# Two PSUM tiles for exp in a selective scan: given out by the framework, or fixed by even and odd number

## The chip, the cores and the metric

The kernel runs on one core of one Trainium2 chip. The core has five engines with instruction queues of their own: TensorE (PE, with its weight loads as PEld), VectorE (DVE), ScalarE (ACT), GpSimd (POOL) and SyncE (SP), which here only issues DMA transfers. Each engine works through its queue in order, and waits on semaphores for what other engines produce or set free. The metric is the device time of one execution in microseconds; lower is better.

## The reference, cut to what matters

The input x has the shape 2 x 256 x 256 x 128. The first layer is a row attention; the second is a state space layer with a selective scan. Only the second matters here. Each image has L = 65,536 positions, 256 inner channels and 16 states per channel:

```python
dA = jnp.exp(delta[:, :, :, None] * A[None, :, None, :])
dBx = (delta * xs)[:, :, :, None] * jnp.transpose(Bs, (0, 2, 1))[:, None]
...
def step(h, inp):
    dA_t, dBx_t, c_t = inp
    h = dA_t * h + dBx_t
    return (h, jnp.einsum('bdn,bn->bd', h, c_t))
...
y = jnp.moveaxis(ys, 0, 2)
return y + Ds[None, :, None] * xs
```

For each channel and state there is a first-order recurrence along the positions: h = dA * h + dBx. The output is the sum over states of h times C. Around it lie a projection, a 3 x 3 depthwise convolution, silu, softplus, a layer norm, a gate and an output projection.

## The kernel before

An image is cut into 64 steps of 4 rows, T = 1024 positions, so that there are 128 steps. In a step the 256 channels x 16 states are 4096 recurrences, 128 partitions of which make a unit: NU = 32 units a step. A unit t goes through these pieces:

```python
POOLED = (4, 7, 10, 13, 16, 19, 24, 26, 31)
...
ps_d = ctx.enter_context(tc.tile_pool(name="ps_d", bufs=2, space=PSUM))
...
def pooled(t):
    return t % NU in POOLED

def decay(t):                                   # ScalarE: da = exp(delta * A), into PSUM
    k, h, m, q = unit(t)
    da = units[t]["da"] = ps_d.tile([P, T], F32, name="da")
    g = h * NQ + q
    nc.scalar.activation(
        da, spreads["delta", k, h, q], AF.Exp, scale=a_neg[:, g, m : m + 1]
    )

def drive(t):                                   # GpSimd: hb = (delta * x) * B, into SBUF
    ...
    hb = s5.tile([P, T], F32, name="hb")
    nc.gpsimd.tensor_tensor(hb, spreads["du", k, h, q], repeats["bb", k, h, m], ALU.mult)

def scan(t):                                    # VectorE: the recurrence
    ...
    u["h"] = u["hb"] if pooled(t) else u["da"]  # written over one of its inputs
    nc.vector.tensor_tensor_scan(u["h"], u["da"], u["hb"], st, ALU.mult, ALU.add)

def remember(t):                                # ScalarE: the last position, for the next step
    ...
    nc.scalar.copy(st, units[t]["h"][:, T - 1 : T])

def product(t):                                 # h * C, on GpSimd for nine units of 32
    ...
    u["yc"] = s8.tile([P, T], F32, name="yc")
    eng = nc.gpsimd if pooled(t) else nc.vector
    eng.tensor_tensor(u["yc"], u["h"], repeats["cc", k, h, m], ALU.mult)
```

A tile da is 128 x 1024 in fp32[...]. [...]in the nine pooled units the scan writes over hb in SBUF, and GpSimd takes the product. In these units da is used up when the scan ends. In the other 23 the scan writes over da, and da is in use until the product and the copy of the last position are done.

The loop sets the order of the queues; what a line below issues stands in its engine's queue in this order:

```python
for t in range(min(slots), max(slots) + 1):
    if 0 <= t + AHEAD < end:
        fetch(t + AHEAD)
    ...
    if 0 <= t + 2 < end:
        drive(t + 2)
    if 0 <= t - 1 < end and pooled(t - 1):
        product(t - 1)
    if 0 <= t + 1 < end:
        decay(t + 1)
    if 0 <= t < end:
        scan(t)
        if not pooled(t):
            product(t)
    if 0 <= t - 5 < end and (t - 5) % NQ == 0:
        add_up(t - 5)    # PE: sums yc over the states
    if 0 <= t - 6 < end and unit(t - 6)[2:] == (NSG - 1, 0):
        y_out(t - 6)     # ScalarE: copies the sum out
    for piece, args in slots.pop(t, ()):
        piece(*args)
    if 0 <= t < end:
        remember(t)
```

The `slots` hold the other work, spread over the units: for the step after the next the projection, convolution (`conv`, `conv_out`, line 515), gate (`gate`, `gate_out`, line 540), silu, B and C (`states`), delta (`size`, `softplus`), and for the step before the layer norm (`turn`: yt, `stats`, `scales`: rstd, `norm`, `back`, `affine`), the gate (`gated`: yg), the output projection (`mix`: o_ps) and its exit (`leave`: ob). ScalarE takes all evictions of these from PSUM. Softplus and silu use another activation table than exp does: a table load stands ahead of each and another one after it.

Of the kernel before, what the change touches and what calls it, by code (L numbers as in the profile page):

```python
# [8 lines left out]
F32 = mybir.dt.float32  # L9
# [3 lines left out]
PSUM = bass.MemoryType.PSUM  # L13
DRAM = bass.MemoryType.DRAM

P = 128
# [5 lines left out]
def attn_then_ssm_kernel(  # L22
# [108 lines left out]
    with tc.tile_pool(name="prep", bufs=1) as prep, tc.tile_pool(  # L131
        name="prep2", bufs=3
# [95 lines left out]
    with tc.tile_pool(name="st", bufs=2) as stp, tc.tile_pool(  # L228
        name="st_x", bufs=3
# [179 lines left out]
    T = R * W  # L409
# [11 lines left out]
    s3 = ctx.enter_context(tc.tile_pool(name="s3", bufs=3))  # L421
    s5 = ctx.enter_context(tc.tile_pool(name="s5", bufs=5))
    s8 = ctx.enter_context(tc.tile_pool(name="s8", bufs=8))
    ps_d = ctx.enter_context(tc.tile_pool(name="ps_d", bufs=2, space=PSUM))
    ps_y = ctx.enter_context(tc.tile_pool(name="ps_y", bufs=1, space=PSUM))
    ps_p = ctx.enter_context(tc.tile_pool(name="ps_p", bufs=1, space=PSUM))
    ps_f = ctx.enter_context(tc.tile_pool(name="ps_f", bufs=1, space=PSUM))
# [312 lines left out]
    units = {}  # L740

    def unit(t):

        k, i = divmod(t, NU)
        h, i = divmod(i, NM)
        m, q = divmod(i, NQ)
        return k, h, m, q
# [26 lines left out]

    def decay(t):
        k, h, m, q = unit(t)
        da = units[t]["da"] = ps_d.tile([P, T], F32, name="da")
        g = h * NQ + q
        nc.scalar.activation(  # L779
            da, spreads["delta", k, h, q], AF.Exp, scale=a_neg[:, g, m : m + 1]  # L780
        )
# [70 lines left out]
    with tc.manual_schedule(engines=engines):  # L852
# [3 lines that stand above are left out]
            if 0 <= t < end and t % (NU * NSTEP) == 0:  # L856
                st = s1.tile([P, NCG, NSG], F32, name="state")
                nc.gpsimd.memset(st, 0.0)
                states_of[steps[t // NU][0]] = st
# [11 lines that stand above are left out]
                add_up(t - 5)  # L871
            if 0 <= t - 6 < end and unit(t - 6)[2:] == (NSG - 1, 0):
                y_out(t - 6)
# [4 lines that stand above are left out]
# [37 lines left out]
```

## Time and profile before

| | |
|---|---|
| time, median of 3 | 18009.35 us (18005.79 to 18027.44) |
| profiled span | 17983.9 us |
| DVE busy | 15218.5 us, 85% |
| PE busy | 14262.3 us, 79% |
| POOL busy | 13400.1 us, 75% |
| ACT busy | 11112.9 us, 62% |
| mean granted TensorE clock | 0.906 of full speed |
| start of the first and of the last scan | 3,497.9 and 17,923.1 us |

The shares mix two parts. Until about 3,500 us the first layer runs, with GpSimd nearly idle; then the 128 steps of the scan follow, with DVE and POOL near full. Within the scan stage (3,490 to 17,930 us, 14,440 us long) DVE is busy for 13,247 us, POOL for 13,358, PE for 11,152, and ACT for 9,567. Busy times count from an instruction's start to its end, and neighbours overlap by up to 0.1 us, so that an engine without gaps shows a little over 100%.

In the groups of instructions, a row holds the line, the engine and the operation, out<-in with shapes and count, then busy time and the mean of one in ns, and last the idle time of the engine just before these instructions with what ended most of it.

### The profile page before, as it was taken

The numbers are of one execution on the slowest core, as the hardware profiler recorded it, in microseconds if no ns is written. First come the engines' busy times: TensorE is split into PE (matmuls) and PEld (weight loads), VectorE is DVE, ScalarE is ACT, GpSimd is POOL, SyncE is SP. The second block draws the span as 40 slices with busy tenths as digits, with TensorE's granted clock in tenths as the row PEclk, the third lists the DMA queues.
The fourth block names the chain that finished last, engine by engine and source line by source line (L and its number), as shares of the span: only waits on it lengthen the run. The fifth ranks groups of instructions, "written<-read, shape, count | busy, mean of one in ns | idle before, by whom it ended". The sixth has DMA issues, their size and how long they took to land. (4 is left out here: it accounts for less than half of the span.)

```text
span 17983.9 us, 178799 instructions
## 1 busy us (share of the span) xinstructions
PE 14262.3 (79%) x56375; PEld 6982.8 (39%) x56375; DVE 15218.5 (85%) x12864; ACT 11112.9 (62%) x19870; POOL 13400.1 (75%) x7084
## 2 busy tenths in 40 slices
PE   4999999777777777777777777777777777777776
PEld 3666666433333333333333333333333333333333
DVE  6555555499999999999999999999999999999998
ACT  2444444466666666666666666666666666666665
POOL 0000000299999999999999999999999999999998
PEclk7999999888899999999999888889888899999887
DMA  4122122266666666666666666666666666666664
GB/s 190 65 71 71 57 71 71 92 220 218 218 221 220 221 221 221 221 221 221 220 220 221 221 219 219 220 220 221 221 220 218 219 221 220 220 220 220 220 219 170
DMA packets 1426641, 3452.04 MB, mean 192 GB/s; under 512 B 119788, under 2 KB 710936, under 8 KB 1407256
## 3 DMA queue, kind: packets, MB, share of 16 engines
q1 hardware_dynamic: 1416984, 3373.49, 54.7%
q0 software_dynamic: 8704, 67.11, 0.9%
q8 instruction: 443, 7.26, 0.2%
q14 instruction: 510, 4.18, 0.1%
HBM read 2752.28 MB, written 687.88 MB: 191 GB/s over the span
## 5 line engine op out<-in xcount | busy, mean ns | idle before, releaser
L787 POOL TENSOR_TENSOR hb<-du_r,bb 128x1024 f32<-128x1024 f32 x4096 | 9566.1, 2360 | 0.0
L794 DVE TENSOR_TENSOR_SCAN da<-da,state,hb 128x1024 f32<-128x1024 f32 x2944 | 6912.4, 2348 | 1064.3 <-ACT da L779 749.3
L779 ACT ACTIVATE da<-delta_r,a_neg 128x1024 f32<-128x1024 f32 x4096 | 4575.5, 1117 | 1155.2 <-DVE hb L794 1086.4
L504 PE MATMUL u_ps<-xn,w_tap 128*128 128x512 f32 x9216 | 4218.6, 603 | 332.3 <-ACT sz L540 242.8
L806 DVE TENSOR_TENSOR yc<-da,cc 128x1024 f32<-128x1024 f32 x2944 | 3605.0, 1225 | 254.2 <-DVE da L794 4.6
L806 POOL TENSOR_TENSOR yc<-hb,cc 128x1024 f32<-128x1024 f32 x1152 | 2714.5, 2356 | 818.9 <-issue 411.9
L794 DVE TENSOR_TENSOR_SCAN hb<-da,state,hb 128x1024 f32<-128x1024 f32 x1152 | 2697.4, 2342 | 15.6 <-ACT da L779 15.3
L826 PE MATMUL y<-yc,sel 128*32 128x512 f32 x16384 | 2469.9, 671 | 280.5 <-POOL yc L806 274.1
L504 PEld LDWEIGHTS u_ps<-xn,w_tap 128*128 128x128 f32 x9216 | 1710.5, 192 | 2348.3 <-issue 1764.8
L398 POOL DMA_DIRECT2D x<-x1g x32 | 23.2, 725 | 3035.0 <-DVE x1g L366 3035.0
L656 PE MATMUL yt<-centre,ys 128*128 128x256 f32 x4096 | 1226.0, 452 | 798.1 <-ACT ob L726 797.0
L799 ACT COPY state<-da 128x1 f32<-128x1 f32 x2944 | 461.2, 157 | 2209.2 <-DVE yc L806 2206.7
L656 PEld LDWEIGHTS yt<-centre,ys 128*128 128x128 f32 x4096 | 895.4, 226 | 1200.8 <-ACT ob L726 992.0
L691 PE MATMUL yd<-ident,yn 128*128 128x128 f32 x2048 | 382.0, 317 | 1126.6 <-ACT yn L680 955.7
L826 PEld LDWEIGHTS y<-yc,sel 128*32 128x32 f32 x16384 | 477.0, 115 | 1973.1 <-issue 1263.9
L552 PE MATMUL xd_ps<-xs,w_xp 128*64 128x512 f32 x1024 | 602.2, 720 | 314.9 <-ACT state L799 174.4
L691 PEld LDWEIGHTS yd<-ident,yn 128*128 128x128 f32 x2048 | 273.3, 160 | 1407.7 <-ACT yn L680 993.9
L570 PE MATMUL dt_ps<-xd,w_dt 8*128 8x512 f32 x1024 | 608.5, 675 | 191.0 <-ACT xd L565 184.1
L515 ACT ACTIVATE xs<-u_ps,cb_c 128x512 f32<-128x512 f32 x512 | 349.6, 683 | 617.8 <-PE u_ps L504 342.5
L318 ACT ACTIVATE e<-s_ps,nmx 128x256 f32<-128x256 f32 x1024 | 472.5, 473 | 355.1 <-DVE nmx L314 354.6
L598 POOL TENSOR_TENSOR xs<-delta,xs 128x1024 f32<-128x1024 f32 x256 | 603.7, 2358 | 40.5 <-ACT delta L589 39.2
L716 PEld LDWEIGHTS o_ps<-w_out,yg 128*128 128x128 f32 x4096 | 604.7, 212 | 35.6
(134 smaller groups left out, 18144.6 us busy)
## 6 DMA issues: line engine op xcount, KB each, us to landing
bb<-bc_d SPq DMA_DIRECT2D x1024, 512.0 KB, 4.2
cc<-bc_d SPq DMA_DIRECT2D x1024, 512.0 KB, 5.2
delta_r<-delta_d SPq DMA_DIRECT2D x1024, 512.0 KB, 5.6
du_r<-du_d SPq DMA_DIRECT2D x1024, 512.0 KB, 4.1
xs_d<-xs SPq DMA_DIRECT2D x128, 1024.0 KB, 3.9
xr<-xs_d SPq DMA_DIRECT2D x256, 512.0 KB, 5.1
delta_d<-delta SPq DMA_DIRECT2D x128, 1024.0 KB, 7.2
du_d<-xs SPq DMA_DIRECT2D x256, 512.0 KB, 3.1
```

Source lines behind the costliest of these rows:

```text
L504: nc.tensor.matmul(o["u"], w_tap[:, h, 3 * dy + dx, :], o["xn"][:, i * RB + dy : i * RB + dy + RB, dx : dx + W], start=(dy == 0 and dx == ...
L552: nc.tensor.matmul(o["xd_ps"], w_xp[:, h, :], o["xs"][:, h, i * TB : (i + 1) * TB], start=(h == 0), stop=(h == NH - 1),)
L570: nc.tensor.matmul(o["dt"], w_dt[:, h, :], o["xd"][0:DR, i * TB : (i + 1) * TB], start=True, stop=True,)
L598: nc.gpsimd.tensor_tensor(du, o["delta"][:, h, :], du, ALU.mult)
L656: nc.tensor.matmul(o["yt"][:, j, :], ys[k, h][:, t0 + j * P : t0 + (j + 1) * P], centre[:, (1 - h) * P : (1 - h) * P + DI], start=(h == 0) ...
L691: nc.tensor.transpose(o["yd"][:, h, j * P : (j + 1) * P], o["yn"][:, j, h * P : (h + 1) * P], ident,)
L716: nc.tensor.matmul(o["o"][:, j, :], o["yg"][:, h, j * P : (j + 1) * P], w_out[:, h, :], start=False, stop=(j == WT - 1 and h == NH - 1),)
L779: nc.scalar.activation(da, spreads["delta", k, h, q], AF.Exp, scale=a_neg[:, g, m : m + 1])
L787: nc.gpsimd.tensor_tensor(hb, spreads["du", k, h, q], repeats["bb", k, h, m], ALU.mult)
L794: nc.vector.tensor_tensor_scan(u["h"], u["da"], u["hb"], st, ALU.mult, ALU.add)
L806: eng.tensor_tensor(u["yc"], u["h"], repeats["cc", k, h, m], ALU.mult)
L826: nc.tensor.matmul(y[q * CQ : (q + 1) * CQ, cols], sel, units[t + q]["yc"][:, cols], start=False, stop=(m == NSG - 1),)
```

## The change

Before, both tiles da come from a pool with two buffers under one name; when a unit asks for one, the framework gives it a buffer that it holds to be free. After the change there are two names with one buffer each, da0 for units of even number and da1 for odd ones, so that a unit always follows the one two before it in its buffer, and the two always alternate. PSUM use stays the same.

```diff
-    ps_d = ctx.enter_context(tc.tile_pool(name="ps_d", bufs=2, space=PSUM))
+    ps_d = ctx.enter_context(tc.tile_pool(name="ps_d", bufs=1, space=PSUM))
...
-        da = units[t]["da"] = ps_d.tile([P, T], F32, name="da")
+        da = units[t]["da"] = ps_d.tile([P, T], F32, name=f"da{t % 2}")
```

It is meant to let the exp of a unit be computed while the scan of the unit before still runs on the other tile.

## The prediction, made before the changed kernel was run

> **What bounds the kernel now.** I read the page first: busy shares, then the 40 slices, then the costliest groups. The page as a whole says that VectorE is the fullest engine, and the slices say where to look: from slice 10 on (about 3,500 us) VectorE and GpSimd are both at 9. That is the scan stage; the ones before it belong to the attention part, which the change does not touch.
>
> ```profile
> PE 14262.3 (79%) x56375; PEld 6982.8 (39%) x56375; DVE 15218.5 (85%) x12864; ACT 11112.9 (62%) x19870; POOL 13400.1 (75%) x7084
> DVE  6555555499999999999999999999999999999998
> POOL 0000000299999999999999999999999999999998
> L787 POOL TENSOR_TENSOR hb<-du_r,bb 128x1024 f32<-128x1024 f32 x4096 | 9566.1, 2360 | 0.0
> L794 DVE TENSOR_TENSOR_SCAN da<-da,state,hb 128x1024 f32<-128x1024 f32 x2944 | 6912.4, 2348 | 1064.3 <-ACT da L779 749.3
> L779 ACT ACTIVATE da<-delta_r,a_neg 128x1024 f32<-128x1024 f32 x4096 | 4575.5, 1117 | 1155.2 <-DVE hb L794 1086.4
> ```
>
> There are 4096 scans, 32 in each of 128 steps. The row to look at is the scan into da: 1064.3 us of idle VectorE before it, ended by ScalarE. And the exp (line 779) itself sat 1086.4 us behind a scan into hb. ScalarE waits for VectorE, and then VectorE for ScalarE: that is a handshake in series, not a full engine. The list of VectorE's waits, cut to the scan stage (3,490 to 17,930 us; columns: total us, times, longest), confirms it:
>
> ```profile
> DVE da L794 <- ACT da L779: 749.3, 514, 149.3
> DVE da L794 <- ACT state L799: 313.5, 249, 1.6
> DVE hb L794 <- ACT da L779: 15.3, 12, 2.0
> ```
>
> The first line holds one wait of 149.3 us, the start of the stage; without it the three lines come to 928.8 us. The timeline shows one such wait, VectorE first, then ScalarE in the same microseconds (columns: start, duration, in brackets the idle before and its releaser):
>
> ```profile
> 9038.63 1.23 DVE L806 TENSOR_TENSOR yc<-da,cc 128x1024 f32<-128x1024 f32 x1
> 9039.77 2.34 DVE L794 TENSOR_TENSOR_SCAN hb<-da,state,hb 128x1024 f32<-128x1024 f32 x1
> 9043.36 2.36 DVE L794 TENSOR_TENSOR_SCAN da<-da,state,hb 128x1024 f32<-128x1024 f32 x1 [1.25 <-ACT state L799]
> ...
> 9040.55 0.59 ACT L540 COPY sz<-z_ps 128x512 f32<-128x512 f32 x1 [1.93 <-PE z_ps L529]
> 9041.03 0.17 ACT L799 COPY state<-da 128x1 f32<-128x1 f32 x1
> 9042.14 1.12 ACT L779 ACTIVATE da<-delta_r,a_neg 128x1024 f32<-128x1024 f32 x1 [0.95 <-DVE hb L794]
> 9043.20 0.17 ACT L799 COPY state<-hb 128x1 f32<-128x1 f32 x1
> ```
>
> The scan of unit 7 (into hb, since 7 is in POOLED) ends at 9042.11. Only then does the exp of unit 8 start; it ends at 9043.26, and scan 8 starts 0.10 later. The wait is booked on the state copy, which ended near it, but its length is that of the exp. Where nothing is missing, the next scan starts 2.26 us after the start of a scan into hb (9030.35 to 9032.61); here it is 3.59. So one such wait costs 1.33 us.
>
> I then numbered the scans of the whole stage by unit and summed the waits over 0.3 us: unit 0 155 us (124 times), 8 157 (125), 11 158 (126), 14 157 (125), 20 158 (126), 23 116 (125), all others 26: together 928. A step takes 112.77 us (median), and five of its units pay 1.25 us each, one 0.93.
>
> [...] the state copy, which only reads da, waits for the product, which only reads it too (ScalarE's waits: 2206.7 us, 1727 times). [...] GpSimd's product takes 2360 ns throughout[...]
>
> **The change part by part.** No instruction is added, and the order on ScalarE, VectorE, PE and GpSimd stays[...]. In the program as built before, the exp of units 8, 11, 14 and 20 of each step, and of unit 0 (in nearly every step), gets the tile of the unit just before it: 626 times in all. Those units follow 7, 10, 13, 19 and 31, all pooled: their da is free when their scan ends, and the framework hands that one out again. After the change no exp does that. The 626 exps wait for the state copy of two units earlier, which is ahead of them on ScalarE; the wait for the scan moves to the copy of hb, after the exp. The 626 are the five units of the table.
>
> What each unit gains, from the step that starts at 9015.52:
> - Units 11, 14, 20: the copies before their exps end at 9050.82, 9062.13 and 9082.86, and the scans they ran behind end at 9053.48, 9064.19 and 9084.92. An exp needs 1.12, so it is hidden with at least 0.7 us to spare. Gain 3 x 1.33 = 4.0.
> - Unit 8: the copy ends at 9041.20 (it stood behind an eviction that waited for PE). The exp would run to 9042.35, scan 8 to start at 9042.45 rather than 9043.36. Gain 0.9; 0.4 stays.
> - Unit 0: behind softplus, its table loads and two evictions the copy ends at 9125.93. The exp would run to 9127.07, the scan start at 9127.17 instead of 9128.16. Gain 1.0; 0.35 stays.
> - Unit 23: two table loads, a silu of 1.91 us and two exps lie in series; this is not the change's matter. But the block begins behind stats, which wait for PE's yt, which waits for the row before to leave (ob); that leaves behind exp 20, earlier now. My choice: 0.3.
>
> Sum 6.2 us a step. Against it I set 0.2, an allowance: PE's stretch from 9023.4 to 9081.2 holds only 3.8 us of idle, VectorE wants it 4 us shorter, and two evictions (units 13 and 14) would then come within 0.1 to 0.7 us of delaying an exp. Net 6.0, so a step of 106.8. Times 128 steps: 768 us. 18009 - 768 = 17241; **predicted 17,240 us**.
>
> **The rivals.**
> - GpSimd becomes the bound. Its work in a step: 32 products at 2.325 when back to back (four took 9.30), 74.4; 9 more for pooled units, 20.9; 2 for du, 4.6; four pairs for rstd, 4.0; copies and memsets, 1.2: 105.1 us. VectorE without any wait: 112.64 - 5 x 1.33 - 0.92 = 105.1 too. So neither can go below 105.1, a gain of 7.7 x 128 = 980 us and 17,030 us. In my walk hb is ready at least 2.2 us before its scan (3.6 now) in every unit. Against it as the bound: at 106.8 GpSimd still has 1.7 us of slack a step.
> - PE becomes the bound through ScalarE's evictions. For: PE is the engine with hardly a gap between units 2 and 18, and ScalarE holds exps behind evictions in one queue; a lower granted clock (0.90 now) would sharpen it. Against: PE waits freely later in the step (5.26 us at 9086.4). If units 8, 14, 15 and 16 each lost 0.4 us more, the step would be 108.4 and the time 17,450.
> - The waits are only moved: the exp no longer waits for the scan, but something else lets ScalarE reach it just as late. For: that is so in part at units 0 and 8. Against: at 11, 14 and 20 ScalarE stood idle for 2.7, 2.1 and 2.1 us before the exp, with nothing but the scan to wait for. If all else failed these three alone make 4.0 x 128 = 510 us, 17,500.
> - Transfers: the stage moves 219 GB/s with its DMA engines busy 0.64 of the time; 6% more is small, and VectorE has no wait on a DMA in the list. No change.
>
> **Range and chances.** Low end: the floor of 17,030 plus a little, since two engines that both run at 105.1 cannot both be free of waits: 17,080. High end: the PE rival, 17,450. Slower than 17,650 (2%) would need over half of the gain to vanish, though the three largest gains have 0.7 us or more to spare: 5%. Slower by 2% would need a new wait of some 9 us a step (360 us over 128 steps, after the gain is gone): 1%.
>
> **What the new profile should show.** If right: the exp's idle behind "DVE hb L794" falls from 1086.4 to under 100 us; idle before the scan into da falls from 1064.3 to 250 to 400 (149 of it the start), what is left standing at units 0, 8 and 23; the state copy takes over waits on the scan into hb; scan, exp and product keep their mean times; GpSimd's idle before its yc falls from 818.9 to under 400. Steps come at 106 to 107 us. Wrong, if scan means grow (then overlap has a cost of its own), if VectorE waits for GpSimd's hb (first rival), or if ScalarE's evictions wait longer for PE and new waits show at units 12 to 17 (second).

## The result, and the profile after

The changed kernel takes **17251.17 us** (median of 4 runs, 17216.71 to 17265.45) against 18009.42 us for the kernel before on the same chip: a ratio of 0.9574, 95% interval 0.9558 to 0.9591. That is 4.3% faster; the prediction said 17,240 us.

From the page of the changed kernel, the busy shares, then two rows of the 40 slices, then the groups (busy us and mean ns of one, then the idle time before them and its main releaser):

```profile
PE 14319.6 (83%) x56375; PEld 6940.5 (40%) x56375; DVE 15182.0 (88%) x12864; ACT 11143.6 (65%) x19870; POOL 13393.4 (78%) x7084
DVE  6555555489999999999999999999999999999998
POOL 0000000089999999999999999999999999999998
...
L794 DVE TENSOR_TENSOR_SCAN da<-da,state,hb 128x1024 f32<-128x1024 f32 x2944 | 6904.3, 2345 | 324.7 <-ACT da L779 321.5
L779 ACT ACTIVATE da<-delta_r,a_neg 128x1024 f32<-128x1024 f32 x4096 | 4576.9, 1117 | 88.7 <-ACT state L799 0.8
...
L806 POOL TENSOR_TENSOR yc<-hb,cc 128x1024 f32<-128x1024 f32 x1152 | 2718.9, 2360 | 201.8 <-issue 156.4
L794 DVE TENSOR_TENSOR_SCAN hb<-da,state,hb 128x1024 f32<-128x1024 f32 x1152 | 2697.9, 2342 | 70.3 <-ACT da L779 70.3
```

The work of one instruction stays within 4 ns: scan 2345 (2348 before), exp 1117 in both, GpSimd's product 2360 (2356). What went is idle time. The exp no longer waits for a scan into hb at all (1086.4 us before), and the idle before the scan into da fell from 1064.3 to 324.7. But the scan into hb, which had 15.6 us, has 70.3: that was not expected. In VectorE's waits of the scan stage (total us, times, longest):

```profile
DVE da L794 <- ACT da L779: 321.5, 319, 151.4
DVE hb L794 <- ACT da L779: 70.3, 38, 2.4
```

Of the first line one wait of 151.4 us is the start of the stage. The rest by unit, in us over the whole stage, start left out; what was predicted to be left stands between. Waits of 0.1 us or more count here. The prediction counted those over 0.3, which would hide unit 0 after the change, where nearly all of 121 waits are shorter:

| unit | before | predicted left | after |
|---|---|---|---|
| 0 | 155 | 45 | 32 |
| 8 | 157 | 51 | 67 |
| 11, 14, 20 | 473 | 0 | 0 |
| 23 | 116 | 80 | 0 |
| 15, 16 (allowance) | 0 | 26 | 0 |
| 28 to 31 | 26 | 26 | 143 |
| sum | 928 | 228 | 243 |

So the sum came out right, though two rows that were put wrong cancel: unit 23 lost its wait altogether, and units 28 to 31 got one. A step now takes 105.98 us in the median (112.77 before) and 107.11 in the mean (112.80): 36 of 127 steps take 108 to 112 us, nearly all others 105.7 to 106.4. The mean difference, 5.70 us, times 128 steps is 730 us; the two profiled executions differ by 720. (The first scan of the kernel before starts at 3,494.3 us; the 3,497.9 in its table is the second.)

Unit 8 in the timeline of the changed kernel, VectorE, then ScalarE (start, duration, in brackets the idle before and its releaser):

```profile
8660.79 2.34 DVE L794 TENSOR_TENSOR_SCAN hb<-da,state,hb 128x1024 f32<-128x1024 f32 x1
8663.45 2.36 DVE L794 TENSOR_TENSOR_SCAN da<-da,state,hb 128x1024 f32<-128x1024 f32 x1 [0.32 <-ACT da L779]
...
8661.57 0.59 ACT L540 COPY sz<-z_ps 128x512 f32<-128x512 f32 x1 [1.93 <-PE z_ps L529]
8662.05 0.17 ACT L799 COPY state<-da 128x1 f32<-128x1 f32 x1
8662.25 1.12 ACT L779 ACTIVATE da<-delta_r,a_neg 128x1024 f32<-128x1024 f32 x1
```

The exp now starts 0.03 after the copy of two units earlier, with scan 7 still running until 8663.13. What is left is the gate eviction (line 540) ahead of it, which waits for TensorE.

### The profile page after: what moved, and what is told of

Its sections match the earlier page's. It is cut to its first block, busy times and chain, and to the rows that moved or that the text cites. A ratio compares the mean times of both kernels' runs of the same rounds, so it can differ in the third digit from the quotient of the medians.

```text
span 17263.7 us, 178676 instructions
## 1 busy us (share of the span) xinstructions
PE 14319.6 (83%) x56375; PEld 6940.5 (40%) x56375; DVE 15182.0 (88%) x12864; ACT 11143.6 (65%) x19870; POOL 13393.4 (78%) x7084
## 5 line engine op out<-in xcount | busy, mean ns | idle before, releaser
L794 DVE TENSOR_TENSOR_SCAN da<-da,state,hb 128x1024 f32<-128x1024 f32 x2944 | 6904.3, 2345 | 324.7 <-ACT da L779 321.5
L779 ACT ACTIVATE da<-delta_r,a_neg 128x1024 f32<-128x1024 f32 x4096 | 4576.9, 1117 | 88.7 <-ACT state L799 0.8
L806 POOL TENSOR_TENSOR yc<-hb,cc 128x1024 f32<-128x1024 f32 x1152 | 2718.9, 2360 | 201.8 <-issue 156.4
L794 DVE TENSOR_TENSOR_SCAN hb<-da,state,hb 128x1024 f32<-128x1024 f32 x1152 | 2697.9, 2342 | 70.3 <-ACT da L779 70.3
L826 PE MATMUL y<-yc,sel 128*32 128x512 f32 x16384 | 2528.0, 681 | 236.9 <-POOL yc L806 230.1
L656 PE MATMUL yt<-centre,ys 128*128 128x256 f32 x4096 | 1068.2, 406 | 226.4 <-ACT ob L726 225.4
L552 PE MATMUL xd_ps<-xs,w_xp 128*64 128x512 f32 x1024 | 687.2, 809 | 480.9 <-ACT state L799 373.1
L656 PEld LDWEIGHTS yt<-centre,ys 128*128 128x128 f32 x4096 | 791.6, 200 | 608.4 <-ACT ob L726 390.2
L570 PE MATMUL dt_ps<-xd,w_dt 8*128 8x512 f32 x1024 | 690.1, 757 | 261.3 <-ACT xd L565 254.4
L699 ACT ACTIVATE yd<-yd,lnb_c,lng_c 128x256 f32<-128x256 f32 x1024 | 542.8, 530 | 149.2 <-PE yd L691 127.8
```

Source lines behind the costliest of these rows:

```text
L552: nc.tensor.matmul(o["xd_ps"], w_xp[:, h, :], o["xs"][:, h, i * TB : (i + 1) * TB], start=(h == 0), stop=(h == NH - 1),)
L570: nc.tensor.matmul(o["dt"], w_dt[:, h, :], o["xd"][0:DR, i * TB : (i + 1) * TB], start=True, stop=True,)
L656: nc.tensor.matmul(o["yt"][:, j, :], ys[k, h][:, t0 + j * P : t0 + (j + 1) * P], centre[:, (1 - h) * P : (1 - h) * P + DI], start=(h == 0) ...
L699: nc.scalar.activation(o["yd"][:, h, :], o["yd"][:, h, :], AF.Identity, bias=lnb_c[:, h : h + 1], scale=lng_c[:, h : h + 1],)
L779: nc.scalar.activation(da, spreads["delta", k, h, q], AF.Exp, scale=a_neg[:, g, m : m + 1])
L826: nc.tensor.matmul(y[q * CQ : (q + 1) * CQ, cols], sel, units[t + q]["yc"][:, cols], start=False, stop=(m == NSG - 1),)
```

## Experiments on the cause

Times are medians, and ratios are to the kernel before on the same chip. Differences in us are between medians from different chips, on which the kernel before took 17,994 to 18,012 us; the four executions of the changed kernel themselves spread over 49 us, and waits by unit come from one execution each. In the first four runs a rule in `decay` chooses the tile:

```diff
+    REPEAT = (0, 8, 11, 14, 20)     # differs from run to run
+    which = {-1: 1}
-        da = units[t]["da"] = ps_d.tile([P, T], F32, name=f"da{t % 2}")
+        which[t] = which[t - 1] if t > 0 and t % NU in REPEAT else 1 - which[t - 1]
+        da = units[t]["da"] = ps_d.tile([P, T], F32, name=f"da{which[t]}")
```

**The old order under the new names** (`REPEAT = (0, 8, 11, 14, 20)`).

> Two names with one buffer each, as in the changed kernel, but units 0, 8, 11, 14 and 20 of every step take the tile of the unit just before them, as they did in the kernel before. If the order of the two tiles at these five units is the whole effect, the time is that of the kernel before: 18,009 us, within 30. If the way the pool gives tiles back (two buffers under one name against two names) has a part of its own, it stays clearly below, under 17,950.

18019.9 us (17998.2 to 18061.36); ratio 1.0009 (1.0002 to 1.0016). The whole gain is the order of the tiles at five units of 32. The 0.1% over the kernel before fits the count: this rule makes 639 repeats, the framework had made 626, and 13 x 1.33 is 17 us.

**Four more repeats** (all nine units after a pooled one).

> As the changed kernel, but after all nine pooled units the next one takes the same tile: 0, 5, 8, 11, 14, 17, 20, 25, 27. Theory: each repeat puts one exp in series, and the four new ones (5, 17, 25, 27) have exps that are on time now, so each costs 1.33 us: 18,009 + 4 x 1.33 x 128 = 18,690 us. Rival: the framework picked this tile where it cost nothing to wait, or other engines' slack takes it up: 18,009 to 18,300 us.

18873.71 us, ratio 1.0482 (1.0466 to 1.0498). The four new waits came as expected, at units 5, 17, 25 and 27, each 1.25 us in every step, and the scan starts 3.60 us after the one before it in place of 2.26. The exp's row of that kernel shows all nine:

```profile
L783 ACT ACTIVATE da<-delta_r,a_neg 128x1024 f32<-128x1024 f32 x4096 | 4579.5, 1118 | 2407.9 <-DVE hb L798 2357.3
```

The cost is larger than the 681 us of the four: against the run with five repeats it is 854. Some 135 us of the rest are longer waits at units 29 to 31 (59 us there with five repeats, 194 here). They go with the granted TensorE clock: between scans 25 and 29 it was below 0.70 in 86 of 124 steps here, and in 15 with five repeats, and those 86 steps hold all but 0.3 us of the waits. What such a clock does there is the subject of the next section. The rival, that other engines' slack takes new repeats up, is wrong.

**Repeats at units 0 and 8 only.**

> As the changed kernel, but units 0 and 8 take the tile of the unit before. Theory: at these two a part of the wait was never the tile's, as ScalarE reaches the exp late in any case; they give back only what they gained, 0.99 and 0.93 us: 1.92 x 128 = 246 us, 17,497 us. Rival: what is left at 0 and 8 after the change is a new wait, and a repeat costs the full 1.34 at each on top: 343 us, 17,594 us.

17424.44 us, ratio 0.9678 (0.9664 to 0.9692), 173 us over the changed kernel where 246 were expected and the rival said 343. By unit the theory holds: unit 0 got 127 us back and unit 8 97 us, with 3.60 us from scan to scan again at both. But the waits at 28 to 31 were 103 us in this execution, not 143. Whether a slower VectorE leaves them less, or this is chance from one execution to the next, is not shown.

**A repeat at unit 20 only.**

> As the changed kernel, but unit 20 of each step takes the tile of unit 19. Theory: scan 20 starts 1.34 us later (3.60 for 2.26 after scan 19), and the wait at unit 23 of some 0.95 us, gone after the change, comes back with it, because the row's exit (ob) stands behind exp 20 on ScalarE, yt behind ob, stats behind yt, and the silu block behind stats: 2.29 us a step, 293 us, 17,544 us. Rival: the wait at 23 went for another reason, as PE ran at another clock there: 1.34 x 128 = 172 us, 17,423 us, and no wait at 23.

17396.63 us, ratio 0.9665 (0.9648 to 0.9681): 145 us over the changed kernel, well under the theory's 293. It is under the rival's 172 too, but by no more than the intervals leave open. The profile has three parts: unit 20 waits 161 us (1.26 in each step), unit 23 waits again, but only in 81 of 128 steps, 60 us in all, and units 28 to 31 wait 49 us instead of 143. Both the theory and the rival for unit 23 thus hold in part, and TensorE's timeline shows how. First yt (turn, in slot 19) in the kernel before, then in the changed kernel, then in two steps of this run:

```profile
9086.43 3.65 PE L656 MATMUL yt<-centre,ys 128*128 128x256 f32 x8 [5.26 <-ACT ob L726]
```

```profile
8913.13 1.99 PE L656 MATMUL yt<-centre,ys 128*128 128x256 f32 x8 [1.16 <-ACT ob L726]
```

```profile
8847.40 3.38 PE L656 MATMUL yt<-centre,ys 128*128 128x256 f32 x8 [3.24 <-ACT ob L726]
...
9063.46 1.99 PE L656 MATMUL yt<-centre,ys 128*128 128x256 f32 x8 [3.23 <-ACT ob L726]
```

The eight matmuls are the same. After 5.26 us of idle TensorE they took 3.65 us, after 1.16 us 1.99. Before the change they took 3.4 to 3.8 us in all of 124 steps in which they start behind scan 20; after it they took 1.99 in 124 of 127. After 3.23 us they took anything from 1.99 to 3.78. The granted clock follows: in the four rows above it was 0.54, 1.00, 0.58 and 1.00 while yt ran.

In the scan stage of the changed kernel the granted clock is 1.0 or 0.5 and nothing else, and all of its 846 changes lie on one grid of 3.41 us. In the run with the repeat at unit 20, the place on its grid goes with what yt takes after 3.23 us: 1.99 us in all 21 steps where yt starts 1.5 to 1.95 us after a grid point, 3.37 to 3.78 in all 41 where it starts up to 1.15 us after one. Stretches at 0.5 came behind gaps of 3.23 us in that run, and behind gaps of 2.3 to 2.7 in the changed kernel (further below).

That yt causes the wait shows step by step: unit 23 waits in none of the 21 steps in which yt took 1.99 us, and 0.8 us on average in the 54 in which it took 3.45 or more. So unit 23 gained twice. Before, and again with the repeat at unit 20, yt starts 0.25 us after scan 20, and 3.78 us of yt leave a wait of 1.05. In the changed kernel exp 20, and ob behind it, come earlier, and yt starts 0.48 us before scan 20. In later runs with this early start and a slow yt (two of those below with an earlier convolution), 3.78 us of yt leave 0.35. The fast yt removes what remains.

## Experiments on what is left

**Keep TensorE busy where it waits.** The same clock would explain the 36 long steps. Between scans 25 and 29, the granted clock was 0.50 to 0.64 in each of the 36, and above 0.72 in all the others but two at the ends of the stage. In one of them (first fence), beside an ordinary step (second), TensorE in units 25 to 28 of the changed kernel:

```profile
9252.52 2.07 PE L570 MATMUL dt_ps<-xd,w_dt 8*128 8x512 f32 x2
9254.52 1.22 PE L713 MATMUL o_ps<-xres,ident 128*128 128x256 f32 x2
...
9259.38 3.78 PE L656 MATMUL yt<-centre,ys 128*128 128x256 f32 x8
```

```profile
9146.94 1.49 PE L570 MATMUL dt_ps<-xd,w_dt 8*128 8x512 f32 x2
9148.36 0.70 PE L713 MATMUL o_ps<-xres,ident 128*128 128x256 f32 x2
...
9150.93 1.99 PE L656 MATMUL yt<-centre,ys 128*128 128x256 f32 x8
```

In both, gaps of 2.7, 0.7 or 0.8 and 2.3 us come before, while TensorE waits for silu and the xd evictions. In the first, all is nearly twice as long for 14 us (four times 3.41); the evictions of delta on ScalarE stand behind it, softplus with its table loads (1.28 us each) behind them, and VectorE pays at units 30 and 31:

```profile
9266.56 2.36 DVE L794 TENSOR_TENSOR_SCAN da<-da,state,hb 128x1024 f32<-128x1024 f32 x1 [1.40 <-ACT da L779]
...
9272.26 2.35 DVE L794 TENSOR_TENSOR_SCAN hb<-da,state,hb 128x1024 f32<-128x1024 f32 x1 [2.01 <-ACT da L779]
```

The test adds matmuls with a zero weight into the running sum y, which do not change it:

```diff
+        def warm(n):
+            for _ in range(n):
+                nc.tensor.matmul(
+                    outs["y"][0:CQ, 0:TB], zsel, w_tap[:, 0, 0:4, :], start=False, stop=False
+                )
...
         at(t, silu_xs)                  # t is slot 21
+        if k >= 2:                      # also around each call below
+            at(t, warm, 2)
         at(t + 1, states, 0)
+            at(t + 1, warm, 1)
         at(t + 2, states_out, 0)
         at(t + 2, states, 1)
+            at(t + 2, warm, 2)
```

> The changed kernel plus five matmuls a step with a zero weight (128x32), added into the sum y, which they leave as it is: two in slot 21, one in 22, two in 23, where TensorE waits for ScalarE (gaps of 2.7, 0.8 and 2.3 us in the profile of the changed kernel). They are 4.3 us more TensorE work a step. Theory: the waits left at units 28 to 31 (143 us in all, in a quarter of the steps) come from TensorE dropping to a slower clock after these gaps, so that the matmuls of delta, o_ps and yt take nearly twice as long and softplus starts late on ScalarE. Kept busy, it stays fast: waits at 28 to 31 under 40 us, about 17,150 us. Rival: ScalarE is too crowded there whatever TensorE does; no gain, or a loss for the added work, 17,250 to 17,350 us.

**17093.33 us**, ratio 0.9497 (0.9484 to 0.951), faster than the changed kernel (the intervals don't overlap) with 4.3 us more TensorE work a step (ten instructions, 0.43 us from one start to the next). The waits at 28 to 31 went from 143 us to 0.3, no step of 127 takes more than 106.4 us, and the means of the matmuls that follow the gaps fell. Groups of the changed kernel, then of this one:

```profile
L570 PE MATMUL dt_ps<-xd,w_dt 8*128 8x512 f32 x1024 | 690.1, 757 | 261.3 <-ACT xd L565 254.4 <-ACT delta L581 6.9
L552 PE MATMUL xd_ps<-xs,w_xp 128*64 128x512 f32 x1024 | 687.2, 809 | 480.9 <-ACT state L799 373.1 <-ACT xd L565 101.4 <-ACT xs L523 6.4
```

```profile
L572 PE MATMUL dt_ps<-xd,w_dt 8*128 8x512 f32 x1024 | 578.5, 645 | 63.6 <-ACT xd L567 56.3 <-ACT delta L583 7.3
L554 PE MATMUL xd_ps<-xs,w_xp 128*64 128x512 f32 x1024 | 497.6, 608 | 326.5 <-ACT state L813 185.4 <-ACT xd L567 134.7 <-ACT xs L525 6.4
```

The granted clock says it outright. In the table by stretches (bounds and length, then busy us of the engines, last granted clock, DMA share, GB/s) the long step of the changed kernel stood at 0.54, and its ordinary step, after 3.41 us at 0.50, at 1.00. The stretch with the same matmuls in a step of this run stood at 1.00 throughout:

```profile
9249.00:9264.00 15.00, 15.00 (x42) 6.97 (x40) 14.49 (x10) 7.28 (x15) 13.75 (x9) 0.54 0.64 228
9144.31:9147.72 3.41, 3.41 (x17) 0.81 (x10) 3.32 (x4) 1.57 (x3) 3.41 (x3) 0.50 0.80 254
9147.72:9161.38 13.66, 8.70 (x44) 4.20 (x42) 13.43 (x8) 11.07 (x18) 13.49 (x11) 1.00 0.74 251
```

```profile
9160.00:9190.00 30.00, 25.80 (x108) 10.00 (x108) 29.38 (x18) 22.66 (x41) 28.54 (x17) 1.00 0.58 180
```

Why the clock stays at 0.5 for 3.41 us in some steps and for four times that or more in others, after the same gaps, is not shown.

**The same matmuls elsewhere**, in slots 8, 9 and 10:

> The same five zero-weight matmuls a step as before, but in slots 8, 9 and 10, where TensorE has hardly a gap. Theory of the clock: they do nothing for the stretch at units 21 to 28, so the waits at 28 to 31 stay near 143 us, and the added work pushes the evictions of the convolution back: 17,250 us or more, up to 17,500. Rival: the gain came from something that five more matmuls bring wherever they stand (another phase between the engines): 17,100 us here as well.

17806.23 us, ratio 0.9895 (0.9878 to 0.9911): 555 us slower than the changed kernel, and 306 over the upper end of what was expected. The waits at 28 to 31 stay (113 us), and 402 us at unit 14 and 154 at unit 15 are new: the squares of yt (`stats`) ahead of exp 14 now wait 4.75 us for TensorE (0.78 in the changed kernel), and the conv eviction ahead of exp 15 waits 3.11. So it is where they stand that counts; where TensorE has hardly a gap, 4.3 us more work cost about as much as it takes.

**The convolution one slot later, alone and with the zero-weight matmuls** (`t = base + 2` becomes `t = base + 3` ahead of the loop over `conv`):

> The changed kernel with the convolution and gate of the step after the next one slot later (first at slot 3 of the step, not 2). Theory: what is left at unit 8 (67 us, 0.54 each) is the first gate eviction, which stands ahead of exp 8 on ScalarE and waits for TensorE; one slot later it stands behind exp 8, and the wait goes: 17,185 us. Rival: TensorE has no room, the chain ends later everywhere and the silu block at slot 21 starts late, or the conv eviction that now stands there waits as long: 17,250 us or more.

> Both edits, the zero-weight matmuls and the slot's shift. Theory: the gains add up, as they are at other units of the step: 17,085 us, with only unit 0 still waiting (0.3 us a step). Rival: the floor of GpSimd and VectorE, 105.1 us a step or some 17,030 us, is near, and their coupling gives some of it back: 17,150 us.

17717.63 us, ratio 0.9843 (0.9829 to 0.9857), and 17596.53 us, ratio 0.9777 (0.9764 to 0.9791). Both theories fell, and the rival of the first held. Unit 8 waits 513 us in the first, 4.1 a step instead of 0.5: the conv eviction in slot 6 now stands ahead of exp 8, and it waits 5.60 us for TensorE, where the gate's waited 1.93. ScalarE's waits for all conv evictions of the stage, in the changed kernel and then in the first of these two:

```profile
ACT xs L515 <- PE u_ps L504: 914.5, 378, 2.8
```

```profile
ACT xs L515 <- PE u_ps L504: 1595.1, 503, 7.1
```

In the second run the matmuls still removed the waits at 28 to 31 (93 us to 0.3).

**One slot earlier** (`t = base + 1`), likewise:

> The changed kernel with the convolution and gate one slot earlier (first at slot 1 of the step, not 2). Moving it later put a conv eviction ahead of exp 8, which waited for TensorE. Theory: earlier, the evictions of slots 4 and 5 stand ahead of exps 6 and 7, both after units that leave time, and none stands ahead of exp 8: its wait (0.54 us a step, 67 us) goes, 17,185 us. Rival: TensorE comes out of the row's work too late to use the slot; the evictions wait as long and now stand ahead of exp 11 or 14, whose scans follow short units: 17,300 us or more.

> Zero-weight matmuls in slots 21 to 23 and the convolution one slot earlier. Theory: both gains add up, 17,093 - 52 (what is left at unit 8 with the matmuls) = 17,040 us, next to the floor of 105.1 us a step. Rival: as for the earlier convolution alone, 17,140 us or more.

17621.55 us, ratio 0.9791 (0.9776 to 0.9805), and 17448.88 us, ratio 0.9694 (0.9679 to 0.9708). The wait at unit 8 is gone as expected, but the conv eviction of slot 12 comes to stand ahead of exp 14 and waits 1.74 us for TensorE, after `stats` ahead of it has waited 2.72 (0.78 in the changed kernel). Unit 14, after a short pooled unit, waits 352 us (361 in the second). That is what the rival had said.

**Only the first of the four groups earlier**, with the matmuls (`t = base + 1`, and `t += 5` after the first group):

> The zero-weight matmuls in slots 21 to 23, and of the four convolution and gate groups only the first one slot earlier (slot 1); the other three stay at slots 6, 10 and 14. Theory: the gate eviction leaves the place ahead of exp 8, and no conv eviction comes to stand ahead of exp 14, so the 52 us left at unit 8 go and nothing comes: 17,040 us. Rival: TensorE's stretch has no room even for this; a wait at unit 6, 7 or 10 takes its place: 17,093 us or more.

17095.43 us, ratio 0.9492 (0.9479 to 0.9505), the same as with the matmuls alone. Unit 8 no longer waits (52 us with the matmuls alone), units 6 and 23 do (34 and 22 us), so the rival held. VectorE's mean step is 105.77 us here and 105.78 there, 0.7 over the 105.1 that the prediction gave as the floor; that is what its waits still add up to (89 and 85 us).

## Why the prediction was right, point by point

- **The bound and the mechanism: right.** A handshake in series, one exp behind a pooled scan at five units of a step. The old order under the new names gives the old time, and four repeats more cost 1.25 us of wait each again.
- **1.33 us for such a wait: right.** 3.60 to 2.26 us from scan to scan at units 11, 14 and 20, with no wait left there.
- **Units 8 and 0: right in kind, off by 0.1 each.** Left are 0.52 us a step at unit 8 (0.4 predicted) and 0.25 at unit 0 (0.35). That the rest was never the tile's is shown by the run with these two repeats.
- **Unit 23: wrong in size.** The step that failed is "My choice: 0.3", put in without a working. The path was right, but the move alone is worth 0.7: yt starts 0.48 us before scan 20 instead of 0.25 after it. It also took yt's 3.65 us as given. TensorE's gap is shorter now, and yt takes 1.99. All of the 0.93 went.
- **The allowance of 0.2 for PE: wrong in place, size and cause.** It looked for new waits behind the evictions of units 13 and 14, where TensorE is full; there were none. They came at units 28 to 31, 0.9 us a step, where TensorE waits most: there the granted clock stood at 0.50 to 0.64 in the 36 long steps, and with the gaps filled by zero-weight matmuls the waits fell from 143 us to 0.3. The second rival was thus real in its path (PE's matmuls, ScalarE's evictions, exps behind them), but named the full stretch. One of its signs did show: the conv evictions waited for PE 914.5 us in the stage, where they had waited 276.3 before. But no scan of units 12 to 17 came to wait for them. It even counted the free time later in the step as a point against.
- **The sum: right, in part by luck.** The terms for unit 23 and for PE are off by 0.6 to the good and 0.7 to the bad, which is why 17,240 came within 11 us of 17,251. It was closer than its terms were.
- **GpSimd as the bound: not reached, right.** Its idle before yc is 201.8 us (818.9 before, under 400 predicted). But the floor is near: with the matmuls, 105.8 us a step against 105.1.
- **Transfers: no part, right.** They went from 219 to 231 GB/s in the scan stage, and VectorE's waits show none on a transfer.

## What to carry to other kernels

When the engine that should be full has the same gap again and again, look at which buffer the blocked instruction was given, not only at how many there are. Here there were two before and after, and their order alone cost 4.3%. And when a stage gets shorter, work out anew the times of the matmuls in it: here the duration of the same eight went with the gap ahead of them and its place on the grid of the clock (1.99 to 3.78 us), and an engine that is not the bound held the bound up through a third engine's queue (143 us at units 28 to 31).

## What was not expected of the hardware

- Eight matmuls of yt took 1.99 us after an idle gap of 1.16 us, 3.65 after 5.26, and after 3.23 anything between 1.99 and 3.78, by the place of their start on a grid of 3.41 us. Stretches at half clock lasted up to 20.5 us with TensorE at work all along (from 6,041.6 us of the changed kernel, six times 3.41: busy for 20.50 us, granted clock 0.50).
- Work that computes nothing made the kernel faster: 4.3 us a step of zero-weight matmuls took 158 us off (17251 to 17093), since they fill gaps; the same work in a full stretch cost 555 us.
